# Stores later in SP's queue, resting rings, and three tiles for the experts' sums in a four-layer kernel

## The chip, the cores and the metric

The kernel runs on one core of a Trainium2 chip. The metric is the device time of one execution in microseconds (us); before the change its median over three runs is 5413.93 us. A difference of less than about 0.2% (11 us) can't be told from none.

The core has five engines that run side by side and wait for each other by semaphores: PE (TensorE, matmuls and transposes), DVE (VectorE), ACT (ScalarE), POOL (GpSimd) and SP (SyncE), which here only issues DMAs. Each takes its instructions strictly in the order in which the program put them. An instruction that has to wait holds up all that stand behind it on that engine. For SP this means: a DMA that waits for its data, or for its tile, holds up every DMA behind it, whatever those are for.

## What is computed

Four layers, each added to its input, on a tensor of 4 images, 384 channels and 48 x 48 places, all in float32. Each layer first normalises its input over 32 groups of channels.

```python
# layer 0: a selective scan over the 2304 places of an image
xz = xs @ in_proj_w.T;  xin, z = split(xz)
xin = silu(conv1d(xin) + conv_b)                    # 4 taps
dt, Bm, Cm = split(xin @ x_proj_w.T);  dt = softplus(dt @ dt_proj_w.T + b)
h_t = exp(dt_t * A) * h_(t-1) + dt_t * B_t * x_t    # 768 channels x 16 states
y_t = sum over states of h_t * C_t
out = layer_norm((y + xin * D) * silu(z) @ out_proj_w.T)
# layer 1: 1x1 conv, filter of 8x8 patches in Fourier space, 3x3 depthwise conv,
#          gelu(first half) * second half, 1x1 conv
# layer 2: 11x11 depthwise conv with kernels made from 4 points
# layer 3: 4 experts, each relu(w1 x + b1), then w2, weighted by a router's top 2
```

## The kernel before, in words

**Scans.** Layer 0 sets the frame. The 2304 places of an image are cut into five chunks (460 or 464 wide), so there are 20 chunks over the four images, numbered 0 to 19 here. A chunk has 6 blocks of 128 channels and 16 states, which makes 96 scans: 1920 in all. The program is written out slot by slot, one scan a slot, in a fixed order on each engine (`manual_schedule`). In slot u ACT makes a decay `da` (L942), POOL makes `bu` = u * B (L953) for slot u + 3, DVE scans (`scan`, L966), and either DVE (L986) or POOL (L995) multiplies by C into a tile `g`, which PE adds up by transposing it into `y` (L886). B and C of a state are 230 KB strips, broadcast to all partitions by DMA from a small DRAM tensor `bcd` (`spread`, L930): one of each every second slot, on SP's queue. B has three buffers and C four.

**What runs beside the scans.** Everything else is cut into tasks: Python generators that `yield` the kind of engine they need next. A `Lane` steps its tasks through the slots: at a `yield ("pool",)`, for example, a task goes on in the middle phase of a later slot. Each step takes at least one slot, so `wait(n)` lets n slots pass. A step can also ask that a `Ring` of tiles has one free. This planning happens when the program is built; what it yields is only the order of the instructions.

- `plan` places the tasks of layer 0 for each chunk: `load` of the next chunk's input (`xch`, L731, two buffers), `project` (PE product `pin` L749, ACT copy L762, three DVE sums L768 per block), `gate`, `out_proj`, `layer_norm`, and `residual`, which adds the result to the old chunk's `xch` tile (L1091), takes statistics, and stores it to `x1d` (L1095). The chunk to be loaded takes the tile that `residual` has just stored from.
- `early_z` computes z of images 3 and 2 ahead, in slots of image 0, and stores it to `zd` (L661).
- `later(b)` is layers 1 to 3 up to the router's scores of image b, and runs during the scans of image b + 1, started at slot 42 of that image. Its strips of layer 1 are in `finish_strip` (27 DVE taps L1415, three products L1447, store of `xr`), the bands of layer 2 in `load_band` (L1513) and `windows` (`xb`, L1578, stored to `x3d` at L1582), the router's input in `scores_of` (`xg`, L1649).
- `experts(b)` is layer 3 of image b: four experts, each 16 blocks of 144 places. A block loads `xe` from `x3d` (L1737) and, but for the first expert, the sum so far `ye` from the DRAM tensor `y3d` (L1740), makes two products on PE (`ph` and `pout`, L1750, 18 matmuls each in the trace) with a relu on ACT between (L1766), adds on DVE (L1782, or L1785 for the first expert, which adds in place to its `xe` tile), and stores back to `y3d`, or to `out` after the last expert (L1791). The tasks of an image come behind each other in a second lane.

All layer work of image 3, and whatever is left of image 2's experts, runs behind the last scan. There a chunk's slots are only steps of the lanes. Image 3's own experts come last, in `all_experts` (`ph` L1850, `pout` L1867), and nothing runs beside them.

**Rings.** `Ring(make, n)` hands out n tiles in turn. `done(k)` marks a tile as read, and `free()` tells the planner that the oldest tile is marked. It marks at the moment at which the program's next instruction may stand: for a tile that is stored, just behind the store's issue. The semaphores then see to it that a load into that tile waits on SP until the store has landed.

Of the kernel before, what the change touches and what calls it, by code (L numbers as in the profile page):

```python
# [9 lines left out]
F32 = mybir.dt.float32  # L10
# [6 lines left out]
P = 128  # L17
# [24 lines left out]


class Ring:


    def __init__(self, make, n):
        self.make, self.n, self.read = make, n, []

    def free(self, k=1):  # L50
        return all(self.read[: max(0, len(self.read) + k - self.n)])

# [5 lines left out]
    def done(self, k):  # L58
        self.read[k] = True

# [34 lines left out]
class Lane:  # L95
# [6 lines left out]

    def step(self, phase, slot, at=0):
        for task in self.active:
            if task.ended:
                continue
            kind, weight, ring, when = task.next
            if PHASE.get(kind, 1) != phase or task.after > slot:
                continue
            if weight and self.bound and self.meter.value + weight > self.meter.limit:  # L110
                continue
            if (ring and not ring[0].free(ring[1])) or (when and not when()):
                continue
# [29 lines left out]
def tile_layers(ctx: ExitStack, tc: tile.TileContext, a: dict, out: bass.AP):  # L143
# [31 lines left out]
    def group_norm(st, bank, mean, rstd, name):  # L175
# [14 lines left out]
        def to_channels(src, n, what):  # L190
            ps = bank(f"c{what}{name}")
            for ct in range(CT):
                nc.tensor.matmul(
                    ps[:, n * ct : n * ct + n], lhsT=gexp[:, bass.ts(ct, P)], rhs=src,
                    start=True, stop=True,
                )
            return ps[:, : n * CT]
# [15 lines left out]
    def group_norm_steps(st, ring, mean, rstd, name):  # L213
# [15 lines left out]
        def to_channels(src, n, what):  # L229
            ps, k = ring.take(f"c{what}{name}")  # L230
            for ct in range(CT):
                nc.tensor.matmul(
                    ps[:, n * ct : n * ct + n], lhsT=gexp[:, bass.ts(ct, P)], rhs=src,
                    start=True, stop=True,
                )
            return ps[:, : n * CT], k
# [179 lines left out]
    with ExitStack() as first:  # L416
# [142 lines left out]
        def scans(wk, mm, ring, meter, place, lanes, begin):  # L559
# [9 lines left out]
            def image_stats(b, ct, h):  # L569
                t = wk.tile([P, TT * C], F32, name=f"xs0_{b}_{ct}_{h}", tag="on", bufs=1)  # L570
                half = HW // 2
                nc.sync.dma_start(t[:, :half], a["x"][b, bass.ts(ct, P), bass.ts(h, half)])
                yield from wait(6)
                for k in range(3):
                    yield ("dve",)
                    nc.vector.bn_stats(stats0[:, b % 2, ct, h, k, :], t[:, bass.ts(k, LB)])

            def image_norm(b):
                yield from group_norm_steps(
                    stats0[:, b % 2].rearrange("p c h k s -> p c (h k) s"), ring,  # L580
                    mean0[:, b], rstd0[:, b], f"0_{b}",
                )
# [54 lines left out]
            def early_z(b, t, j):  # L637
# [21 lines left out]
                ring.done(r)  # L659
                yield ("pool",)  # L660
                nc.sync.dma_start(zd[b][bass.ts(j, P), bass.ds(starts[t], n)], z[:, :n])  # L661
# [62 lines left out]

            def load(i):
                (b, t), c = G[i], st[i]
                x = c["x"] = wk.tile(
                    [P, CT, DCONV - 1 + TM], F32, name=f"xch{b}_{t}", tag="xch", bufs=2
                )
                h = DCONV - 1 if t else 0  # L730
                nc.sync.dma_start(  # L731
                    x[:, :, DCONV - 1 - h : DCONV - 1 + CHUNKS[t]],
                    strip(a["x"][b], bass.ds(starts[t] - h, h + CHUNKS[t])),
                )
                return
                yield

# [336 lines left out]
            def residual(i, ct):  # L1074
# [18 lines left out]
                nc.vector.bn_stats(stats1[b % 2][:, ct, t, :], x)  # L1093
                yield ("pool",)
                nc.sync.dma_start(x1d[b][bass.ts(ct, P), bass.ds(starts[t], n)], x)  # L1095
# [172 lines left out]
        def later(b, ring, accr):  # L1268
# [10 lines left out]

            def slots(tag, shape, n):  # L1280

                return Ring(
                    lambda name: d["wk"].tile(shape, F32, name=name, tag=tag, bufs=n), n
                )
# [10 lines left out]
            def begin1():  # L1295
                wk = d["wk"] = stack.enter_context(tc.tile_pool(name=f"l1_{b}", bufs=2))
                d["w_in"] = wk.tile([P, CT, C], F32, name=f"w_in1_{b}", tag="w_in", bufs=1)
                nc.sync.dma_start(d["w_in"], per_channel(a["L1_w_inT"]))
                w = d["w_out"] = wk.tile([P, 2, C], F32, name=f"w_out1_{b}", tag="w_out", bufs=1)
                nc.sync.dma_start(w[:, 0, :], a["L1_w_outT"][:P, :])  # L1300
                nc.sync.dma_start(w[64:P, 1, :], a["L1_w_outT"][P:, :])
                mean = small.tile([P, CT], F32, name=f"mean1_{b}", tag="mean")
# [90 lines left out]
            def finish_strip(hb):  # L1393
# [46 lines left out]
                for ct in range(CT):  # L1440
                    yield ("pe", 1.3, (ring, 1))
                    ps, r = ring.take(f"pb{b}_{hb}_{ct}")
                    nc.tensor.matmul(  # L1443
                        ps[:, :LB], lhsT=w[:, 0, bass.ts(ct, P)], rhs=act[:, 0, :],
                        start=True, stop=False,
                    )
                    nc.tensor.matmul(  # L1447
                        ps[:, :LB], lhsT=w[64:P, 1, bass.ts(ct, P)], rhs=act[64:P, 1, :],
                        start=False, stop=True,
# [97 lines left out]
            def windows(ct, k, r, first, last, final):  # L1547
# [26 lines left out]
                if last:  # L1574
# [5 lines left out]
                    nc.vector.bn_stats(stats3[b % 2][:, ct, k, :], x[:, :n])  # L1580
                    yield ("pool",)
                    nc.sync.dma_start(x3d[b][of_band(ct, k)], x[:, :n])  # L1582
# [38 lines left out]

            xg = slots("xg", [P, CT, LB], 2)

# [64 lines left out]
        def experts(b, ring, rings):  # L1688
# [42 lines left out]
            def load3(s, e):  # L1731
                yield (
                    "pool", 0, None,
                    lambda: rings["xe"].free() and (not e or rings["ye"].free()),
                )
                x = take(("x", s, e), "xe", f"xe{b}_{s}_{e}")
                nc.sync.dma_start(x, strip(x3d[b], bass.ts(s, EB)))  # L1737
                if e:
                    y = take(("y", s, e), "ye", f"ye{b}_{s}_{e}")
                    nc.sync.dma_start(y, strip(y3d, bass.ts(s, EB)))  # L1740
                yield from wait(3)

            def block(s, e):
# [33 lines left out]
                yield ("late",)  # L1777
                key = ("y" if e else "x", s, e)
                x = d[key][0]
                if e:  # L1780
                    y = x.rearrange("p c t -> p (c t)")
                    nc.vector.tensor_add(y, ps[:, : CT * EB], y)  # L1782
                else:
                    for m in range(CT):
                        nc.vector.scalar_tensor_tensor(  # L1785
                            x[:, m, :], ps[:, bass.ts(m, EB)], b2_sum[:, m : m + 1],
                            x[:, m, :], ALU.add, ALU.add,
                        )
                ring.done(r)
                yield ("pool",)  # L1790
                nc.sync.dma_start(strip(out[b] if e == NE - 1 else y3d, bass.ts(s, EB)), x)  # L1791
                done(key)

# [104 lines left out]

        def of_experts(pool, sizes):
            for tag, n in sizes.items():  # L1900
# [4 lines left out]
                    ),  # L1905
                    n,
                )
# [13 lines left out]
        def begin(b):  # L1921
# [9 lines left out]
            first.enter_context(tc.tile_pool(name="experts", bufs=2)),  # L1931
            {"we": 1, "xe": 2, "ye": 2, "hr": 1},
        )
        with (
# [6 lines left out]
            at = place[0]  # L1941
            while not all(ring.read):
                at += 1
# [5 lines left out]
        with (  # L1949
# [135 lines left out]
```

## Time and profile before

The three runs took 5412.89, 5413.93 and 5417.67 us. The profile is of one further execution.

| what | us |
|---|---|
| median of the runs | 5413.93 |
| profiled execution | 5405.14 |
| its span, from first to last instruction | 5403.1 |
| scans, first to last | 86.5 to 4516.4 |
| mean granted TensorE clock, share of full | 0.919 |

How the queries are read. A row of waits names the engine and line that waited, the arrow to what ended the wait, then the total in us, the number of times and the longest. `SPq` is SP's queue, `DMA y3d<-ye` the transfer from the tile ye to y3d. In a timeline a row has start, duration, engine, line, operation, what it writes and reads and how many were merged, and in brackets the idle time before it with what ended it. The rows in tenths are 40 equal slices of the span.

DMAs on SP's queue that matter here, from the list of issues (us from issue to landing, median):

```profile
xe<-x3d SPq DMA_DIRECT2D x192, 216.0 KB, 2.8
ye<-y3d SPq DMA_DIRECT2D x144, 216.0 KB, 2.8
y3d<-ye SPq DMA_DIRECT2D x96, 216.0 KB, 2.2
...
x1d<-xch SPq DMA_DIRECT2D x48, 230.0 KB, 4.2
...
y3d<-xe SPq DMA_DIRECT2D x48, 216.0 KB, 2.7
out<-ye SPq DMA_DIRECT2D x48, 216.0 KB, 4.5
...
x3d<-xb SPq DMA_DIRECT2D x36, 240.0 KB, 3.2
xch<-in_x SPq DMA_DIRECT2D x12, 694.5 KB, 4.5
```

### The profile page before, as it was taken

What the parts mean: (1) busy time and instruction counts of PE and PEld (TensorE: products, weight loads), DVE (VectorE), ACT (ScalarE), POOL (GpSimd) and SP (SyncE); (2) the same over time, 40 slices, a digit from 0 to 9 for tenths busy, and PEclk for the clock granted to TensorE, in tenths of its full rate; (3) what the DMA queues carried; (4) which work ended last, traced back from release to release, by engine and by line L of the source; (5) the groups of instructions that cost most, each with busy time, mean ns of one, the idle gap of its engine ahead of it and who ended that gap; (6) DMA issues with size and microseconds to landing.
All of it is one profiled execution on the core that took longest, in us unless ns stands there. A gap on an engine that the chain in (4) does not pass through costs nothing. (4 is left out here: it accounts for less than half of the span.)

```text
span 5403.1 us, 82006 instructions
## 1 busy us (share of the span) xinstructions
PE 4646.1 (86%) x27796; PEld 3666.7 (68%) x27796; DVE 4067.1 (75%) x5581; ACT 2989.0 (55%) x6632; POOL 3363.1 (62%) x3020
## 2 busy tenths in 40 slices
PE   5898877787768988888889988888799988999899
PEld 3555545454446766765668867665678877889799
DVE  5998899889997888889887778798987875452200
ACT  3566655565547765565567745565477653335321
POOL 3788778886677788876678678775677783000000
PEclk8898987788879999998899999998899999999899
DMA  4565545443344555655566565655566573543210
GB/s 152 172 187 175 178 128 150 129 143 120 111 127 131 148 165 157 191 161 147 149 172 178 161 200 155 173 146 149 154 182 174 158 213 115 175 138 105 64 27 23
DMA packets 648873, 794.36 MB, mean 147 GB/s; under 512 B 60149, under 2 KB 642661, under 8 KB 648062
## 3 DMA queue, kind: packets, MB, share of 16 engines
q1 hardware_dynamic: 638148, 787.38, 49.9%
q8 instruction: 221, 3.62, 0.3%
q10 hardware_dynamic: 10298, 1.67, 0.2%
q14 instruction: 206, 1.69, 0.1%
HBM read 685.04 MB, written 103.81 MB: 146 GB/s over the span
## 5 line engine op out<-in xcount | busy, mean ns | idle before, releaser
L953 POOL TENSOR_TENSOR bu<-u,B 128x460 f32<-128x460 f32 (+1 forms) x1920 | 2227.0, 1170 | 795.5 <-DVE g L966 349.8
L942 ACT ACTIVATE da<-dt,a_neg 128x460 f32<-128x460 f32 (+1 forms) x1920 | 1242.4, 648 | 310.6 <-DVE g L986 185.6
L886 PE MATMUL y<-ident,g 128*115 128x128 f32 (+1 forms) x7680 | 1111.3, 292 | 192.5 <-DVE g L986 114.8
L886 PEld LDWEIGHTS y<-ident,g 128*115 128x115 f32 (+1 forms) x7680 | 991.2, 183 | 400.4 <-DVE g L986 140.5
L995 POOL TENSOR_TENSOR g<-g,C 128x460 f32<-128x460 f32 (+1 forms) x885 | 1030.0, 1164 | 246.8 <-ACT carry L980 244.3
L966 DVE TENSOR_TENSOR_SCAN da<-da,carry,bu 128x460 f32<-128x460 f32 (+1 forms) x828 | 971.7, 1174 | 122.2 <-ACT da L942 76.7
L966 DVE TENSOR_TENSOR_SCAN g<-da,carry,bu 128x460 f32<-128x460 f32 (+1 forms) x708 | 819.8, 1167 | 57.7 <-issue 18.8
L986 DVE TENSOR_TENSOR g<-da,C 128x460 f32<-128x460 f32 (+1 forms) x1035 | 656.4, 634 | 175.7 <-DMA C<-bcd 62.0
L980 ACT COPY carry<-da 128x1 f32<-128x1 f32 x828 | 130.3, 157 | 760.5 <-DVE g L986 758.0
L1750 PE MATMUL pout<-hr,we 128*128 128x144 f32 x3456 | 485.0, 297 | 51.5 <-ACT hr L1766 37.8
L1750 PE MATMUL ph<-xe,we 128*128 128x144 f32 x3456 | 484.7, 298 | 33.6 <-DMA xe<-x3d 18.9
L1750 PEld LDWEIGHTS pout<-hr,we 128*128 128x128 f32 x3456 | 456.3, 197 | 75.3 <-ACT hr L1766 47.9
L1750 PEld LDWEIGHTS ph<-xe,we 128*128 128x128 f32 x3456 | 459.4, 199 | 51.5 <-DMA xe<-x3d 13.7
L1557 PE MATMUL pc<-band,row 128*128 128x162 f32 (+14 forms) x3456 | 451.3, 284 | 11.2 <-ACT row L1544 10.9
L1557 PEld LDWEIGHTS pc<-band,row 128*128 128x128 f32 x3456 | 440.0, 194 | 16.6 <-ACT row L1544 11.9
L749 PE MATMUL pin<-xch,w_inx 128*128 128x463 f32 (+2 forms) x720 | 344.8, 621 | 55.1 <-DMA xch<-in_x 32.3
L1415 DVE SCALAR_TENSOR_TENSOR dw<-pad,w_dw,dw 128x384 f32<-128x384 f32 x576 | 348.0, 615 | 20.4 <-ACT pad L1390 9.6
L1037 PE MATMUL po<-w_out,zs 128*115 128x384 f32 (+1 forms) x960 | 342.2, 499 | 14.7 <-DVE ye L1782 9.3
L1766 ACT ACTIVATE hr<-ph,nb 128x144 f32<-128x144 f32 x576 | 176.2, 376 | 279.2 <-PE ph L1750 278.4
L1524 ACT ACTIVATE rep<-x,br,wr 128x192 f32<-128x192 f32 x576 | 273.7, 540 | 4.2 <-issue 4.2
L768 DVE SCALAR_TENSOR_TENSOR xc<-pin,conv_w,xc 128x460 f32<-128x460 f32 (+1 forms) x360 | 249.2, 692 | 30.7 <-ACT xc L762 18.5
L749 PEld LDWEIGHTS pin<-xch,w_inx 128*128 128x128 f32 x720 | 143.8, 213 | 179.8 <-issue 136.3
(211 smaller groups left out, 5979.2 us busy)
## 6 DMA issues: line engine op xcount, KB each, us to landing
B<-bcd SPq DMA_DIRECT2D x768, 230.0 KB, 3.6
C<-bcd SPq DMA_DIRECT2D x768, 230.0 KB, 4.0
B<-bcd SPq DMA_DIRECT2D x192, 232.0 KB, 3.8
C<-bcd SPq DMA_DIRECT2D x192, 232.0 KB, 4.3
xe<-x3d SPq DMA_DIRECT2D x192, 216.0 KB, 2.8
ye<-y3d SPq DMA_DIRECT2D x144, 216.0 KB, 2.8
y3d<-ye SPq DMA_DIRECT2D x96, 216.0 KB, 2.2
xs<-x1d SPq DMA_DIRECT2D x24, 576.0 KB, 5.2
```

The lines of the kernel that those rows point to most:

```text
L749: nc.tensor.matmul(ps[:, lo : halo + n], lhsT=w_inx[:, k, bass.ts(j, P)], rhs=c["x"][:, k, lo : halo + n], start=k == 0, stop=k == CT - 1,)
L886: nc.tensor.matmul(c["y", m][:w, bass.ts(k, P)], lhsT=src[:, bass.ts(k, w)], rhs=ident, is_transpose=True, start=c["terms", m] == 1 and k ...
L942: nc.scalar.activation(da[:, :n], c["dt", p][:, m % 2, :n], AF.Exp, scale=a_neg[:, m, s : s + 1])
L953: nc.gpsimd.tensor_mul(bu[:, :n], c["u", p][:, m % 2, :n], live["B", u // 2][:, :n])
L966: nc.vector.tensor_tensor_scan(here[:, :n], da[:, :n], bu[:, :n], last if t else nil[:, 0:1], ALU.mult, ALU.add,)
L986: nc.vector.tensor_mul(live["g", u][:, :n], live["h", u][:, :n], live["C", u // 2][:, :n])
L995: nc.gpsimd.tensor_mul(g[:, :n], g[:, :n], live["C", u // 2][:, :n])
L1037: nc.tensor.matmul(ps[:w, :C], lhsT=c["zs"][:, m, bass.ts(k, w)], rhs=w_out0[:, m, :], start=m == 0, stop=m == MT - 1,)
L1415: nc.vector.scalar_tensor_tensor(v, src, w_dw[:, ct, k : k + 1], v, ALU.mult, ALU.add)
L1524: nc.scalar.activation(rep[:, :, n, :, :].rearrange("p g r c -> p r g c"), rows.rearrange("p (r g c) -> p r g c", r=BR, c=BC), AF.Identity ...
L1557: nc.tensor.matmul(d["acc2"][0][:, : BANDS[k] * W].rearrange("p (h w) -> p h w", w=W)[:, lo - edges[k] : hi - edges[k], xlo:xhi], lhsT=d[" ...
L1750: nc.tensor.matmul(ps[:, bass.ts(m, EB)], lhsT=w[:, k, bass.ts(m, P)], rhs=of[:, k, :], start=k == 0, stop=k == CT - 1,)
```

## The change

A ring gets a `rest`: a tile counts as free only `rest` slots after its `done`. The rings of `early` and `xb` and the experts' `ye` in the scans rest two slots, `xg` and the experts' `xe` one. Stores of `zd`, `x1d`, `x3d` and of the experts' sums wait two or three slots, where they waited one, and the load of the next chunk waits two more. In the scans the experts have three `ye` tiles instead of two, and `xb` has four tiles instead of two. The first expert no longer adds in place to its `xe` tile but into a `ye` tile, which it stores; its `xe` tile is free after that sum. Behind the scans the experts' rings have no rest. Room in SBUF comes from two places: the second part of layer 1's `w_out` is kept once, in unused partitions of `gexp`, and `stats0` has one copy instead of two.

```diff
+CLOCK = [0]
 class Ring:
-    def __init__(self, make, n):
-        self.make, self.n, self.read = make, n, []
+    def __init__(self, make, n, rest=0):
+        self.make, self.n, self.read, self.rest = make, n, [], rest
     def free(self, k=1):
-        return all(self.read[: max(0, len(self.read) + k - self.n)])
+        return all(
+            v is not False and v + self.rest <= CLOCK[0]
+            for v in self.read[: max(0, len(self.read) + k - self.n)]
+        )
...
     def done(self, k):
-        self.read[k] = True
+        self.read[k] = CLOCK[0]
...
     def step(self, phase, slot, at=0):
+        CLOCK[0] = slot
...
-    gexp = const("gexp", [GROUPS, C], a["c_gexp"])
+    gexp = cp.tile([P, C], F32, name="gexp")
+    nc.sync.dma_start(gexp[:GROUPS, :], a["c_gexp"])
+    nc.scalar.dma_start(gexp[64:P, :], a["L1_w_outT"][P:, :])
...
-        stats0 = wp.tile([P, 2, CT, 2, 3, 6], F32, name="stats0")
+        stats0 = wp.tile([P, 1, CT, 2, 3, 6], F32, name="stats0")
...
             def early_z(b, t, j):
...
-                yield ("pool",)
+                yield from wait(2)
                 nc.sync.dma_start(zd[b][bass.ts(j, P), bass.ds(starts[t], n)], z[:, :n])
...
             def load(i):
+                yield from wait(2)
...
             def residual(i, ct):
...
-                yield ("pool",)
+                yield from wait(3)
                 nc.sync.dma_start(x1d[b][bass.ts(ct, P), bass.ds(starts[t], n)], x)
...
-                    n,
+                    n, 2,
...
-            xbs = slots("xb", [P, max(BANDS) * W], 2)
+            xbs = slots("xb", [P, max(BANDS) * W], 4, 2)
...
-                    yield ("pool",)
+                    yield from wait(2)
                     nc.sync.dma_start(x3d[b][of_band(ct, k)], x[:, :n])
...
-            xg = slots("xg", [P, CT, LB], 2)
+            xg = slots("xg", [P, CT, LB], 2, 1)
...
             def load3(s, e):
                 yield (
                     "pool", 0, None,
-                    lambda: rings["xe"].free() and (not e or rings["ye"].free()),
+                    lambda: rings["xe"].free() and rings["ye"].free(),
                 )
                 x = take(("x", s, e), "xe", f"xe{b}_{s}_{e}")
                 nc.sync.dma_start(x, strip(x3d[b], bass.ts(s, EB)))
+                y = take(("y", s, e), "ye", f"ye{b}_{s}_{e}")
                 if e:
-                    y = take(("y", s, e), "ye", f"ye{b}_{s}_{e}")
                     nc.sync.dma_start(y, strip(y3d, bass.ts(s, EB)))
-                yield from wait(3)
+                yield from wait(2)
...
-                            x[:, m, :], ps[:, bass.ts(m, EB)], b2_sum[:, m : m + 1],
+                            y[:, m, :], ps[:, bass.ts(m, EB)], b2_sum[:, m : m + 1],
                             x[:, m, :], ALU.add, ALU.add,
                         )
+                    done(("x", s, e))
                 ring.done(r)
-                yield ("pool",)
-                nc.sync.dma_start(strip(out[b] if e == NE - 1 else y3d, bass.ts(s, EB)), x)
-                done(key)
+                yield from wait(2)
+                nc.sync.dma_start(strip(out[b] if e == NE - 1 else y3d, bass.ts(s, EB)), y)
+                done(("y", s, e))
...
-            {"we": 1, "xe": 2, "ye": 2, "hr": 1},
+            {"we": 1, "xe": 2, "ye": 3, "hr": 1}, {"xe": 1, "ye": 2},
...
-            of_experts(wk, {"we": 2, "xe": 3, "ye": 3, "hr": 3})
+            of_experts(wk, {"we": 2, "xe": 3, "ye": 3, "hr": 3}, {})
```

More of the change, by code (lines that the diff above doesn't have):

```diff
@@ L193, in to_channels @@
                 nc.tensor.matmul(
-                    ps[:, n * ct : n * ct + n], lhsT=gexp[:, bass.ts(ct, P)], rhs=src,
+                    ps[:, n * ct : n * ct + n], lhsT=gexp[:GROUPS, bass.ts(ct, P)], rhs=src,
                     start=True, stop=True,
@@ L232, in to_channels @@
                 nc.tensor.matmul(
-                    ps[:, n * ct : n * ct + n], lhsT=gexp[:, bass.ts(ct, P)], rhs=src,
+                    ps[:, n * ct : n * ct + n], lhsT=gexp[:GROUPS, bass.ts(ct, P)], rhs=src,
                     start=True, stop=True,
@@ L575, in image_stats @@
                     yield ("dve",)
-                    nc.vector.bn_stats(stats0[:, b % 2, ct, h, k, :], t[:, bass.ts(k, LB)])
+                    nc.vector.bn_stats(stats0[:, 0, ct, h, k, :], t[:, bass.ts(k, LB)])
             def image_norm(b):
                 yield from group_norm_steps(
-                    stats0[:, b % 2].rearrange("p c h k s -> p c (h k) s"), ring,
+                    stats0[:, 0].rearrange("p c h k s -> p c (h k) s"), ring,
                     mean0[:, b], rstd0[:, b], f"0_{b}",
@@ L734, in load @@
                 )
-                return
-                yield
             def project(i, j):
@@ L1278, in put, with slots @@
                 tasks.append(task)
-            def slots(tag, shape, n):
+            def slots(tag, shape, n, rest=0):
                 return Ring(
-                    lambda name: d["wk"].tile(shape, F32, name=name, tag=tag, bufs=n), n
+                    lambda name: d["wk"].tile(shape, F32, name=name, tag=tag, bufs=n), n, rest
                 )
@@ L1298, in begin1 @@
                 nc.sync.dma_start(d["w_in"], per_channel(a["L1_w_inT"]))
-                w = d["w_out"] = wk.tile([P, 2, C], F32, name=f"w_out1_{b}", tag="w_out", bufs=1)
-                nc.sync.dma_start(w[:, 0, :], a["L1_w_outT"][:P, :])
-                nc.sync.dma_start(w[64:P, 1, :], a["L1_w_outT"][P:, :])
+                w = d["w_out"] = wk.tile([P, C], F32, name=f"w_out1_{b}", tag="w_out", bufs=1)
+                nc.sync.dma_start(w, a["L1_w_outT"][:P, :])
                 mean = small.tile([P, CT], F32, name=f"mean1_{b}", tag="mean")
@@ L1443, in finish_strip @@
                     nc.tensor.matmul(
-                        ps[:, :LB], lhsT=w[:, 0, bass.ts(ct, P)], rhs=act[:, 0, :],
+                        ps[:, :LB], lhsT=w[:, bass.ts(ct, P)], rhs=act[:, 0, :],
                         start=True, stop=False,
@@ L1447, in finish_strip @@
                     nc.tensor.matmul(
-                        ps[:, :LB], lhsT=w[64:P, 1, bass.ts(ct, P)], rhs=act[64:P, 1, :],
+                        ps[:, :LB], lhsT=gexp[64:P, bass.ts(ct, P)], rhs=act[64:P, 1, :],
                         start=False, stop=True,
@@ L1777, in block @@
                 yield ("late",)
-                key = ("y" if e else "x", s, e)
-                x = d[key][0]
+                y = d["y", s, e][0]
                 if e:
-                    y = x.rearrange("p c t -> p (c t)")
-                    nc.vector.tensor_add(y, ps[:, : CT * EB], y)
+                    of = y.rearrange("p c t -> p (c t)")
+                    nc.vector.tensor_add(of, ps[:, : CT * EB], of)
                 else:
@@ L1897, in tile_layers, with of_experts @@
         place = [0]
-        def of_experts(pool, sizes):
+        def of_experts(pool, sizes, rest):
             for tag, n in sizes.items():
@@ L1905, in of_experts @@
                     ),
-                    n,
+                    n, rest.get(tag, 0),
                 )
@@ L1941, in tile_layers @@
             at = place[0]
-            while not all(ring.read):
+            while not ring.free(ring.n):
                 at += 1
```

## The prediction

> **What bounds the kernel now.** I began with the page's totals and slices: no engine is full over the span, so the bound has to be read by stage.
>
> ```profile
> PE 4646.1 (86%) x27796; PEld 3666.7 (68%) x27796; DVE 4067.1 (75%) x5581; ACT 2989.0 (55%) x6632; POOL 3363.1 (62%) x3020
> DVE  5998899889997888889887778798987875452200
> POOL 3788778886677788876678678775677783000000
> ```
>
> The 1920 scans (one is a "slot") run from 86.5 to 4516.4 us, 2.31 us a slot; there DVE and POOL are both 7 to 9 tenths busy. Behind 4516 POOL has nothing to do. From the stretches: 4516 to 4912 (layers 1 of the last image beside image 2's experts) has PE busy 376 of 396 us; 5100 to 5403 is PE alone, untouched by the change. In the scans PE, DVE and POOL lie close: 3125 to 3344 has PE 193, DVE 173, POOL 171 of 219 us. So what counts there is idle time of DVE and POOL. The waits say who causes it; first SP's own queue in the scans (0 to 4516):
>
> ```profile
> SPq L1740 <- DMA y3d<-ye: 185.9, 64, 7.5
> SPq L1791 <- DVE ye L1782: 160.8, 52, 7.6
> SPq L1737 <- DMA y3d<-xe: 138.5, 38, 8.0
> SPq L1513 <- DMA x3d<-xb: 119.2, 39, 5.6
> ...
> SPq L1740 <- DMA out<-ye: 105.9, 28, 7.2
> SPq L661 <- ACT carry L980: 104.3, 36, 7.2
> SPq L731 <- DMA x1d<-xch: 72.8, 19, 5.3
> SPq L1582 <- DVE xb L1578: 68.6, 28, 6.1
> ...
> SPq L1791 <- DVE xe L1785: 46.6, 26, 5.3
> ```
>
> SP stands 1003 us (the sum of these nine) on a store whose data isn't made, or on a load whose tile is still being stored. Behind it in the same queue are the B and C strips of the scan. The timeline shows it, once per expert block:
>
> ```profile
> 4414.77 0.39 SPq L1791 DMA_DIRECT2D out<-ye  x1
> 4415.20 1.38 SPq L1737 DMA_DIRECT2D xe<-x3d  x1
> 4420.96 0.36 SPq L1740 DMA_DIRECT2D ye<-y3d  x1
> 4421.72 0.33 SPq L930 DMA_DIRECT2D B<-bcd  x1
> ```
>
> From 4416.6 to 4421.0 SP issues nothing; DVE's product at 4419.02 had stood idle 3.46 us for its C, and POOL's bu at 4416.97 1.69 us for B. Over 1961 to 4516, where experts run:
>
> ```profile
> DVE g L986 <- DMA C<-bcd: 58.4, 25, 6.1
> ```
>
> POOL idles 93.8 us for B in that stretch, mostly where DVE isn't waiting for it.
>
> **The change, part by part.** I read where each instruction lands from the built order of both kernels; a slot is placed in SP's queue by the B load beside it.
>
> *Stores later, rings resting, three ye tiles.* In the scans, all 92 ye loads that wait for a ye store stood in the store's own slot; now 71 do, each 2 or more slots behind. The 36 xe loads that waited for y3d<-xe are gone (expert 0 writes a ye tile), 39 xb loads become 2 at 4 slots, 18 xch loads move from 0 to 2 slots or more. Two slots are 4.2 us in the experts' stage (2.10 each from 4314 to 4516); the stores land in 2.2 (y3d<-ye), 4.5 (out<-ye) and 3.2 us (x3d<-xb). The Trainium skill, "DMA: Bandwidth & Descriptors", Anatomy of one DMA, prices a transfer at 2.0 us + bytes/436 GB/s: 2.5 us for these 216 KB, so by the rule no wait is left. By the row out<-ye leaves 0.3 us x 28 = 8 us on SP, which its queue hides. I take the row: nearly all 1003 us of SP's standing goes, only the tile xr (61.0 us) stays. What that is worth is DVE's idle time, not SP's: 58.4 for C, and about 9 us of scans late behind a bu that was late for B, makes 67. Another engine is close behind in each stage, so some comes back as another wait: ends 25 (most is retaken by ACT's da, 65.1 us of DVE idle now, and PE) and 95 (POOL's B idle counts as well where POOL sets the pace). I take 70% of 67: **-47 us**, near the row.
>
> *The next chunk's xch load goes later.* x1d stores move from slots 35, 37, 39 to 37, 39, 41, and the load from 39 to 43 in 18 of 19 chunks; the projection that reads it stays at slot 45 on PE, its ACT copy and its three DVE sums (slot 47) behind it in their queues. This is the change's own new wait. Now:
>
> ```profile
> 932.40 0.38 SPq L1095 DMA_DIRECT2D x1d<-xch  x1
> 936.64 0.38 SPq L731 DMA_DIRECT2D xch<-in_x  x1
> 937.08 0.48 SPq L930 DMA_DIRECT2D B<-bcd  x1
> 937.66 0.38 SPq L930 DMA_DIRECT2D C<-bcd  x1
> 939.50 0.32 SPq L930 DMA_DIRECT2D B<-bcd  x1
> 939.87 0.42 SPq L930 DMA_DIRECT2D C<-bcd  x1
> ...
> 942.01 0.32 SPq L930 DMA_DIRECT2D B<-bcd  x1
> ```
>
> The load already waited for its store, and goes at 936.6; in the new order it stands behind the pair of 939.5, so at 940.3, 3.7 us later. PE's pin started at 941.18, when it landed (PE idle 2.67); it would start at 944.9, and DVE's sum, at 946.37 now with 0.90 idle, at 949.9. Everything behind that on DVE, the scan of slot 48 first, waits: 3.7 us. Done so for each chunk (new issue = the later of POOL's second bu of slot 45 + 0.85 us and the third store's landing; less PE's and DVE's slack), chunks 2 to 10 lose 1.6, 1.8, 3.8, 3.7, 1.8, 0, 2.8, 0.9, 1.2, and chunks 11 to 19 nothing, since SP was so late there that the load went at DVE's slot 42 to 45 anyway. Sum **+18 us**; ends 0 (SP ahead of this) and 72 (4.0 us in all 18).
>
> *More blocks in the scans.* Of image 2's 64 expert blocks 57.7 had PE work behind the last scan, now 51.9. About six blocks move into the scans: 6 x 0.6 us DVE (L1782) is 3.6, and 27 us of PE, which has 10 to 30 us idle in each chunk; **+5** (0 to 15).
>
> *Behind the scans.* Six blocks less are 6 x 2 x 2.21 = 26.5 us of PE. But the experts now end during layer 1's strip 4 of the last image, where they ended behind strip 5. So layer 1's end stands alone: 27 taps of 0.615 us for the last strip are 16.6 us of DVE, with gelu and three products some 35 us from strip 4's product to the next norm, against 56 now (4853.7 to 4910). Up to strip 4 there are 5.1 blocks more beside it than before, +22.5. Together +22.5 - 21 = about 0; the start gains 8, since two rounds like this one, store then load into one tile, fall away:
>
> ```profile
> 4506.48 4.19 DMA y3d<-xe
> 4510.69 2.71 DMA xe<-x3d
> ```
>
> **-8** (-26 if all of PE's time counts, +8 if the lone strip is slower).
>
> *The rest.* Early z is spread over slots 63 to 351 (58 to 290 before) with the same work, and is through before slot 480; slots 288 to 480 without it took 1.96 us, 96 to 288 with it 2.01. gexp's second half is one ACT-queue DMA hidden by the 1152 KB loads at the start; four 96 KB w_out loads go. stats0's single copy meets no reader, as image 0's norm is long done. Nothing for these.
>
> Sum: -47 + 18 + 5 - 8 = -32. The profiled execution took 5405.1 us (span 5403.1), so 5373; the runs' median, 5413.9, is 8.8 above it, so I forecast 5414 - 32 = **5382**.
>
> A rule speaks against this: the skill's "Perfetto Trace Analysis", Identifying the Most-Contended Engine, says to optimise the engine of highest occupancy first. That is PE (86%), and PE waits only 16.2 us on xe loads in 1961 to 4516, so the rule prices the gain at 16 and, with pins +18 and blocks +5, the sum at about 0. I follow the row: the scan's chain is in order on DVE, and DVE's 3.46 us at 4419 were lost with PE free.
>
> **Rivals.** (1) *The freed time is retaken*: DVE then waits for ACT's da or PE instead; for it speaks PE's 219 us of 235 in 4079 to 4314. Gain 25 instead of 47: -10, 5404. (2) *The xch load decides, slower*: at slot 45 of 18 chunks PE, ACT and DVE stand behind a later load. The rest of the change nets -50, so this decides from 50/18 = 2.8 us a chunk; at the full 4.0 it is +72, time 5436. For it: chunks 4 and 5 work out at 3.7. Against: SP's lateness in chunks 11 to 19. (3) *POOL's idle counts too*: 95 instead of 47 and pins at 5: -93, 5321; for it POOL's 93.8 us, against it DVE waits little for bu. (4) That the loads still stand behind their stores is ruled out by the order.
>
> **Chances.** Forecast 0.47 (own range 5354 to 5404), rival 1 0.18, rival 2 0.20, rival 3 0.15. The range 5330 to 5436 reaches most of rival 2 and part of 3. Within 0.2% (11 us, what a measurement can tell) lie rival 1 and a little of the forecast's edge, less rival 1's own edge: 0.17; slower 0.20; faster 0.63.
>
> **What would show it.** In the new profile: SP's waits of ye, xe, xb loads on stores near zero in the scans; DVE's idle for C under 20 us; the last scan ending near 4492; PE's wait on xch up from 46 us, with DVE's sums idle at slot 47; fewer than 52 blocks behind the last scan and layer 1's last strip alone. Wrong if C's wait stays, or if slots 40 to 56 of chunks 2 to 10 grow by more than 3 us each.

## The result and the profile after

The changed kernel takes **5445.5 us** (median of 6 runs, 5434.4 to 5452.9), beside 5413.4 for the kernel before on the same chip: a ratio of 1.0066 (95% interval 1.0049 to 1.0083), some 32 us slower. The forecast was 5382, its range ended at 5436. The profiled execution has a span of 5440.7 us; its scans run from 87.9 to 4582.7, 64.9 us longer than before, and what lies behind them takes 858.0 instead of 886.7. So the loss is in the scans, and part of it is won back behind them.

The page's totals and slices, in the order shown of before:

```profile
PE 4661.6 (86%) x27796; PEld 3665.8 (67%) x27796; DVE 4063.9 (75%) x5581; ACT 2983.3 (55%) x6632; POOL 3362.4 (62%) x3020
...
DVE  5988888888997788889897777889897776353200
...
POOL 3778778787676778876677677876677786000000
```

DVE and POOL do the same work as before within 4 us. What grew is idle time in between. SP's own queue over the scans:

```profile
SPq L940 <- POOL bu L963: 2537.3, 843, 14.1
SPq L847 <- ACT xd L843: 137.2, 20, 42.8
SPq L1746 <- PE ph L1759: 92.1, 33, 6.6
SPq L1746 <- DVE ye L1793: 83.2, 32, 5.3
...
SPq L1749 <- DMA y3d<-ye: 35.3, 24, 3.9
...
SPq L1591 <- DVE xb L1587: 18.3, 17, 2.4
SPq L743 <- DMA x1d<-xch: 15.5, 8, 4.1
```

Here the change does what was forecast: the ye loads' 186 us on their stores are 35, the 138 us of the xe loads on y3d<-xe are gone, and SP mostly stands at the first row: the next B strip waiting for its buffer. New is that the xe loads stand 175 us for the readers of their tiles (third and fourth row). DVE's idle time for C, summed over the scans, went from 62 us to 2.6. It didn't help. The groups of the chunk's projection, PE's product and DVE's sum, before:

```profile
L749 PE MATMUL pin<-xch,w_inx 128*128 128x463 f32 (+2 forms) x720 | 344.8, 621 | 55.1 <-DMA xch<-in_x 32.3
L768 DVE SCALAR_TENSOR_TENSOR xc<-pin,conv_w,xc 128x460 f32<-128x460 f32 (+1 forms) x360 | 249.2, 692 | 30.7 <-ACT xc L762 18.5
```

and after:

```profile
L759 PE MATMUL pin<-xch,w_inx 128*128 128x463 f32 (+2 forms) x720 | 349.4, 628 | 101.6 <-DMA xch<-in_x 86.2
L778 DVE SCALAR_TENSOR_TENSOR xc<-pin,conv_w,xc 128x460 f32<-128x460 f32 (+1 forms) x360 | 249.6, 693 | 111.1 <-ACT xc L772 58.9
```

The number behind the second bar is the idle time just before these instructions, and the row's end says what ended most of it. PE stood 32.3 us for xch before and stands 86.2 us now; DVE's idle time before the sum went from 30.7 to 111.1 us, 80 us more, which is more than the scans lost in all.

The place is the one that the prediction showed at 932 to 942 us, in chunk 4. SP's queue there now:

```profile
961.33 0.38 SPq L940 DMA_DIRECT2D C<-bcd  x1
961.76 0.42 SPq L1105 DMA_DIRECT2D x1d<-xch  x1
964.98 0.32 SPq L940 DMA_DIRECT2D B<-bcd  x1
965.39 0.38 SPq L940 DMA_DIRECT2D C<-bcd  x1
965.88 0.38 SPq L743 DMA_DIRECT2D xch<-in_x  x1
967.48 0.32 SPq L940 DMA_DIRECT2D B<-bcd  x1
```

The load stands behind the next B and C pair. PE's product and DVE's sum of that chunk, first before:

```profile
941.18 4.09 PE L749 MATMUL pin<-xch,w_inx 128*128 128x460 f32 x6 [2.67 <-DMA xch<-in_x]
...
946.37 2.16 DVE L768 SCALAR_TENSOR_TENSOR xc<-pin,conv_w,xc 128x460 f32<-128x460 f32 x3 [0.90 <-ACT xc L762]
```

and after:

```profile
969.77 1.17 DVE L976 TENSOR_TENSOR_SCAN g<-da,carry,bu 128x464 f32<-128x464 f32 x1
971.66 4.94 PE L759 MATMUL pin<-xch,w_inx 128*128 128x460 f32 x6 [7.68 <-DMA xch<-in_x]
...
977.70 2.16 DVE L778 SCALAR_TENSOR_TENSOR xc<-pin,conv_w,xc 128x460 f32<-128x460 f32 x3 [6.76 <-ACT xc L772]
979.78 1.18 DVE L976 TENSOR_TENSOR_SCAN da<-da,carry,bu 128x464 f32<-128x464 f32 x1
```

DVE ends a scan at 970.94 and does nothing until 977.70: 6.76 us, where it was 0.90. That is 5.86 us for this chunk. Measured from the scan of slot 34 in both traces, the load was issued 3.76 us later (the prediction had 3.7). But then it took 5.78 us from issue to PE's start, where it had taken 4.54: 1.24 more. And the six matmuls themselves went slower, 4.94 us instead of 4.09: 0.85 more. These three terms, 3.76 + 1.24 + 0.85, are what DVE lost. All this is chunk 4 alone.

The 0.85 us come from PE's clock. The stretch of the six matmuls, before:

```profile
941.18:942.05 0.87, 0.87 (x3) 1.00 1.06 373
942.05:945.46 3.41, 3.41 (x7) 0.50 0.64 212
```

and after:

```profile
971.66:976.60 4.94, 4.94 (x7) 0.50 0.40 109
```

The columns are the stretch and its length, PE's busy time with the number of its matmuls (those that only touch the stretch are counted too), then the granted TensorE clock, the DMA share (of packets that start in the stretch, so it can pass 1) and GB/s. Before, PE began at full clock and was halved 0.87 us into the product, which ended at 945.27; after, it was at half clock throughout. Counted in time at full clock both are the same work: 0.87 + 3.22/2 = 2.48 us, and 4.94/2 = 2.47. In chunk 17 of the changed kernel the six ran at a clock of 1.00 and took 2.57:

```profile
4030.66 2.57 PE L759 MATMUL pin<-xch,w_inx 128*128 128x463 f32 x6 [2.93 <-DMA xch<-in_x]
```

The Trainium skill, "TensorE: Matmul & The Clock Gate", Part 1, says that PE's clock is halved after an idle window of about 3.4 us, and comes back after as long of steady work. The half clock behind 7.68 us of idle time agrees with it. But before, 2.67 us of idle time were enough, and 2.93 us in chunk 17 were not, so here the length of the idle time alone doesn't decide. The page also calls the window free-running, which would make it matter where in it the idle time falls; no run here tests that.

### The profile page after: what moved, and what is told of

Same layout as the page of the kernel before. It is cut to its first block, busy times and chain, and to the rows that moved or that the text cites. A ratio compares the mean times of both kernels' runs of the same rounds, so it can differ in the third digit from the quotient of the medians.

```text
span 5440.7 us, 81940 instructions
## 1 busy us (share of the span) xinstructions
PE 4661.6 (86%) x27796; PEld 3665.8 (67%) x27796; DVE 4063.9 (75%) x5581; ACT 2983.3 (55%) x6632; POOL 3362.4 (62%) x3020
## 5 line engine op out<-in xcount | busy, mean ns | idle before, releaser
L1759 PE MATMUL ph<-xe,we 128*128 128x144 f32 x3456 | 473.5, 293 | 7.1 <-DVE zs L1033 3.4
L759 PE MATMUL pin<-xch,w_inx 128*128 128x463 f32 (+2 forms) x720 | 349.4, 628 | 101.6 <-DMA xch<-in_x 86.2
L778 DVE SCALAR_TENSOR_TENSOR xc<-pin,conv_w,xc 128x460 f32<-128x460 f32 (+1 forms) x360 | 249.6, 693 | 111.1 <-ACT xc L772 58.9
```

The lines of the kernel that those rows point to most:

```text
L759: nc.tensor.matmul(ps[:, lo : halo + n], lhsT=w_inx[:, k, bass.ts(j, P)], rhs=c["x"][:, k, lo : halo + n], start=k == 0, stop=k == CT - 1,)
L1759: nc.tensor.matmul(ps[:, bass.ts(m, EB)], lhsT=w[:, k, bass.ts(m, P)], rhs=of[:, k, :], start=k == 0, stop=k == CT - 1,)
```

## Experiments

Two theories stood at the start. **P**: the cost is the later xch load alone, larger than the +18 of the forecast, and the rest of the change is a gain. **R**: the time that SP's freed queue gives is retaken by other waits all over the scans, and the load is a small part. The first four kernels ran beside the kernel before at 5412.3 us, the next four at 5411.3, the last two at 5413.7, each group on a chip of its own, so times of different groups are set beside each other here.

**1. The load back.** The changed kernel, with the load and the stores of its tile where they stood before:

```diff
             def load(i):
-                yield from wait(2)
+                yield from ()
...
             def residual(i, ct):
...
-                yield from wait(3)
+                yield ("pool",)
                 nc.sync.dma_start(x1d[b][bass.ts(ct, P), bass.ds(starts[t], n)], x)
```

> The changed kernel with two waits taken out again: the x1d stores one slot behind their sums and the next xch load right behind the third, as before; rings, experts and bands as changed. Theory P (the later xch load is the cost: PE's first projection waits, ACT's copy and DVE's three sums stand behind it in their queues): DVE's idle in slots 40 to 52 falls from 135 us to 75 or so, scans end near 4520 instead of 4583, time about 5385, under the kernel before since the experts' stalls are gone and six blocks left the tail. Theory R (what the freed C and B loads gave is retaken by ACT and PE everywhere, and the new order of the lanes costs by itself): the time stays at 5430 or more; slots 40 to 48 explain at most 20 us.

Measured: **5354.4 us**, ratio to before 0.9897 (0.988 to 0.9913). The two lines cost 91 us in the changed kernel, more than the 60 that were expected, and without them it is 58 us faster than before. Chunk 4 of this kernel:

```profile
940.18 0.38 SPq L743 DMA_DIRECT2D xch<-in_x  x1
940.62 0.48 SPq L940 DMA_DIRECT2D B<-bcd  x1
...
944.63 3.78 PE L759 MATMUL pin<-xch,w_inx 128*128 128x460 f32 x6 [2.46 <-DMA xch<-in_x]
```

The load is ahead of the pair again, and PE starts 4.45 us behind its issue. Summed by groups of eight slots, the changed kernel is 82.7 us longer in the scans than this one, and slots 40 to 48 alone make 83.0 of it. Behind the last scan it is 15.0 us longer (858.0 and 843.0). That is more than the 91 in all, because the profile of this kernel is of the fastest of its four runs. The scans are 17.8 us shorter than before, and what lies behind them is 843.0 us, 43.7 less than before. Theory P holds for the scans.

**2. The load alone.** The kernel before, with the two delays and nothing else of the change:

```diff
             def load(i):
+                yield from wait(2)
...
-                return
-                yield
...
             def residual(i, ct):
...
-                yield ("pool",)
+                yield from wait(3)
                 nc.sync.dma_start(x1d[b][bass.ts(ct, P), bass.ds(starts[t], n)], x)
```

> The kernel before with those two waits alone: x1d stores two slots later, next xch load behind two more slots. Theory P: slower by 50 to 70 us (about 5470), with 5 to 7 us more in slots 40 to 48 of chunks 1 to 8 and PE's wait for xch near 90 us; in chunks 9 to 19 less, as SP stands on the experts' stores anyway. Theory R: at most 20 us slower, 5430.

Measured: 5530.6 us, ratio 1.0219 (1.0202 to 1.0236), 118 us slower, where 50 to 70 were expected. PE stands 160.0 us for xch before pin, up to 20.0 at a time. That SP's standing at the experts' loads delays the load still further here is likely, but wasn't tested by itself. So the two parts of the change aren't independent, and the change's other half softens this one: 91 instead of 118.

**3. Which of the two delays.** The changed kernel with only the load's own wait taken out (e4), and with only the stores put back (e7):

```diff
             def load(i):
-                yield from wait(2)
+                yield from ()
```

> The changed kernel with only the load's own two slots taken out: the stores stay two slots later, and the xch load is issued right behind the third store. The load must wait for that store's landing of about 4 us, so it goes at about the same time as in the changed kernel. Theory P with the store as its cause: 5445 within 10 us, PE's wait for xch stays near 90 us, and SP's wait on x1d<-xch is back at 70 us. Theory P with the load's two slots as its cause: 5400 or less. Theory R: no change.

```diff
             def residual(i, ct):
...
-                yield from wait(3)
+                yield ("pool",)
```

> The kernel after with the residual stores back at one slot, the load's own wait of two slots left in. Two slots of the load on top of late stores cost 5445.5 - 5415.5 = 30 us (after against e4_store_late). If the price is one per slot of lateness, the two slots cost about 30 here too: 5385. If there is slack and only the last slots of lateness hurt, the two first slots are nearly free: 5355 to 5365. Idle of PE before pin for xch: 30 us by the first, under 20 by the second.

Measured: 5415.5 (ratio 1.0004, 0.9997 to 1.0011) and 5376.6 (0.994, 0.9924 to 0.9957). From the kernel with neither, the load's wait alone costs 22 us, the stores' alone 61, and the load's wait on top of the stores' 30. For e4 neither of the outcomes named in advance came, for e7 the time lay between them. The load cannot start before the stores of its tile have landed: with the late stores alone SP stands 75.4 us for them at the load, as expected. Chunk 4 of the kernel with the load's wait alone:

```profile
955.52 0.38 SPq L940 DMA_DIRECT2D C<-bcd  x1
956.13 0.38 SPq L743 DMA_DIRECT2D xch<-in_x  x1
...
961.91 4.17 PE L759 MATMUL pin<-xch,w_inx 128*128 128x460 f32 x6 [3.73 <-DMA xch<-in_x]
```

Measured from the scan of slot 36, the load goes at 12.06 us here and at 12.12 in experiment 1: no later at all. Only its place differs, behind the pair instead of ahead of it, and PE starts 5.78 us after the issue instead of 4.45. So 1.3 us of the price in this chunk go with the place in the queue, not with the time of issue. In chunks 1 to 4 this kernel's load, always right behind a pair, takes 1.3 to 2.0 us longer from issue to PE than experiment 1's.

**4. The projection later.** The changed kernel with PE's six projections moved later (the first by three slots, the next four by two or one, the last not at all), which gives the late load its time back (e5), and the same on the kernel of experiment 1 (e6):

```diff
-                            put(45 + 3 * j, ("x", more, j), lambda j=j: project(more, j),
+                            put(48 + 5 * j // 2, ("x", more, j), lambda j=j: project(more, j),
```

> The changed kernel with the next chunk's six projections starting at slot 48 instead of 45 and 2.5 slots apart instead of 3 (they end at slot 60 as before). Theory P: the load has landed when PE reaches the first projection; PE's wait for xch falls under 15 us, DVE's idle in slots 40 to 52 falls by 60 us or more, time about 5375 to 5385. Theory R: within 10 us of the changed kernel, 5445.

> The kernel after with the chunk's load and its residual stores back where they were before (as in e1_load_back, 5354.4) and, besides, the four projections at slots 48, 50, 53, 55 (as in e5_pin_late, 5369.2). If the projection's slot matters only because the load lands late (theory P), nothing is left to gain once the load is early: PE's idle for xch falls from 13 to about 0 and the time is 5340 to 5360. If the later slot is worth something by itself, 5300 to 5335. If the later projections crowd the next chunk's beginning, over 5370.

Measured: 5369.2 (ratio 0.9924, 0.9907 to 0.9941) and 5355.9 (0.9894, 0.9871 to 0.9918). The load may stay where the change put it: with a later reader, PE's idle time for xch falls from 86.2 to 2.5 us, and 76 of the 91 us come back. With the load early there is nothing to gain from it (5354.4 and 5355.9). So the cost in the scans is the distance between the load and its reader, not the load's place beside other work: e5's scans are even 5.6 us shorter than experiment 1's.

The 15 us that don't come back lie behind the last scan, and go with the late stores. The three kernels that have them need 858.0 (the change), 856.6 (e4) and 865.4 us (e5) there; the kernels with the stores back need 842.1 (e7), 843.0 (experiment 1) and 848.9 (e6). In each of the three PE stands for layer 1's last strip, in the changed kernel:

```profile
4935.01 0.91 PE L1456 MATMUL pb<-act,gexp 64*128 64x384 f32 x2
4944.43 1.62 PE L1452 MATMUL pb<-act,w_out 128*128 128x384 f32 x2 [8.50 <-DVE act L1446]
4945.97 1.65 PE L1456 MATMUL pb<-act,gexp 64*128 64x384 f32 x2
```

In e4 and e5 it is 8.15 us, and in the other three no such wait is there. Behind it the same two matmuls take 1.65 us instead of 0.91, at a granted clock of 0.50. How the late stores lead to this is open.

Over the variants of the changed kernel that keep the reader at slot 45 the time goes with PE's idle time for xch before pin:

| kernel | PE idle for xch, us | time, us |
|---|---|---|
| neither delay (1) | 13.0 | 5354.4 |
| load's wait (3) | 31.0 | 5376.6 |
| stores' wait (3) | 57.0 | 5415.5 |
| both: the change | 86.2 | 5445.5 |

From the first row to the last that is 91.1 us for 73.2, or 1.24 us of time for each us that PE stands there.

**5. What gains the other 58 us.** Four kernels from that of experiment 1. In the first the experts' part is undone: two ye tiles, no rest for xe and ye, the first expert's sum in xe, the store at the next step.

```diff
-                    lambda: rings["xe"].free() and rings["ye"].free(),
+                    lambda: rings["xe"].free() and (not e or rings["ye"].free()),
...
-                y = d["y", s, e][0]
+                key = ("y" if e else "x", s, e)
+                x = d[key][0]
...
-                yield from wait(2)
-                nc.sync.dma_start(strip(out[b] if e == NE - 1 else y3d, bass.ts(s, EB)), y)
-                done(("y", s, e))
+                yield ("pool",)
+                nc.sync.dma_start(strip(out[b] if e == NE - 1 else y3d, bass.ts(s, EB)), x)
+                done(key)
...
-            {"we": 1, "xe": 2, "ye": 3, "hr": 1}, {"xe": 1, "ye": 2},
+            {"we": 1, "xe": 2, "ye": 2, "hr": 1}, {},
```

> e1_load_back with the experts' part undone: two ye tiles, no rest for xe and ye, the first expert's sum in its xe tile, the store at the next POOL step, three slots after the load. If the experts carry what the change gains, all 58 us come back: about 5410, with some six more blocks behind the last scan (about 880 us there) and DVE waiting for C again by 20 us and more outside slots 40 to 52. If the gain is that of the xb, x3 and early z parts, it stays near 5365, with 845 to 855 us behind the last scan.

Measured: 5413.0, ratio 1.0004 (0.9993 to 1.0014). All 58 us are the experts'; the xb, xg and early z parts and the room made for the tiles, taken together, show none. Of the two places named for them, the one behind the last scan was only partly met: 862.6 us there, not 880; the scans gave the larger part. DVE's idle time for C came back to 42 us, but only 14 of them lay outside slots 40 to 52, where 20 and more were expected.

The second undoes the xb part:

```diff
-            xbs = slots("xb", [P, max(BANDS) * W], 4, 2)
+            xbs = slots("xb", [P, max(BANDS) * W], 2)
...
-                    yield from wait(2)
+                    yield ("pool",)
                     nc.sync.dma_start(x3d[b][of_band(ct, k)], x[:, :n])
```

> e1_load_back with the xb part undone: two xb tiles, no rest, the x3d store at the next POOL step. If the experts carry the gain, this costs little: 5355 to 5365. If the standing of SP at the xb loads and stores (119 and 69 us in the kernel before) is what cost the scans, 5375 to 5400, the loss in the scans and not behind them.

Measured: 5348.9, ratio 0.9887 (0.987 to 0.9904), not to be told from experiment 1. Yet SP's queue stands again, over the scans:

```profile
SPq L1522 <- DMA x3d<-xb: 115.3, 39, 5.9
SPq L1591 <- DVE xb L1587: 78.3, 33, 5.5
```

194 us of SP's standing at xb, where experiment 1 has 13.5 in the second row. They cost nothing that the time shows: in the profiles the scans are 12.9 us longer and what lies behind them is 6.4 shorter.

The third and fourth split the experts' part: three ye tiles without rests (e10), and the rests with two ye tiles (e11).

```diff
-            {"we": 1, "xe": 2, "ye": 3, "hr": 1}, {"xe": 1, "ye": 2},
+            {"we": 1, "xe": 2, "ye": 3, "hr": 1}, {},
```

> e1_load_back with three ye tiles, but without the rest of the xe and ye rings in the scans: a load may again stand in the step of its tile's store. If SP's standing is what the experts' part took away (my term of -47), SP stands at ye and xe loads again for hundreds of us and the 58 us come back: about 5410. If the third tile and the earlier take, which let a block's loads run ahead of the block before, carry the gain, it stays at 5350 to 5370.

```diff
-            {"we": 1, "xe": 2, "ye": 3, "hr": 1}, {"xe": 1, "ye": 2},
+            {"we": 1, "xe": 2, "ye": 2, "hr": 1}, {"xe": 1, "ye": 2},
```

> e1_load_back with two ye tiles instead of three in the scans, the rest of both rings kept. A ye tile is then out of use for longer in each round, so fewer blocks are done in the scans. If the third tile carries the gain: more PE work behind the last scan (880 us and more there) and 5400 to 5440. If freeing SP is enough: 5355 to 5375.

Measured: 5364.2 (ratio 0.9911, 0.9891 to 0.9931) and 5426.9 (1.0021, 1.0006 to 1.0036). Without the rests 10 us are lost, within the two intervals. This test is weaker than was expected of it: SP stood less than "hundreds of us" more, perhaps since the third tile alone already takes most loads away from their stores. The rows of e10 over the scans:

```profile
SPq L1746 <- PE ph L1759: 226.3, 56, 10.9
SPq L1749 <- DMA y3d<-ye: 115.0, 34, 5.9
```

In experiment 1 they are 95.8 and 24.9 us: 221 us more of standing for about 10 us. The third tile, on the other hand, is worth 72 us where the rests are kept (5426.9 - 5354.4). Two tiles without rests, in experiment e8, take 5413.0. Where the third tile acts is seen from the experts' two products on PE, counted up to the last scan and behind it; first experiment 1:

```profile
0.00:4499.10 4499.10, 702.22 (x5055) 666.04 (x5056) 0.91 0.55 160
4499.10:4899.10 400.00, 241.76 (x1860) 232.72 (x1858) 0.98 0.49 145
```

then two tiles with rests:

```profile
0.00:4495.80 4495.80, 639.91 (x4395) 605.25 (x4396) 0.91 0.54 157
```

The number of matmuls is in brackets behind PE's time. A block is 36 matmuls, so 660 fewer are 18 blocks that didn't fit beside the scans. The scans themselves end at nearly the same time, and what lies behind takes 932.9 us instead of 843.0. In this pair a block beside the scans costs next to nothing; behind them it costs PE's full time.

## Why the prediction was wrong

**The term that failed is the +18 of "The next chunk's xch load goes later".** It measured 91 us against the rest of the change; in the profiles 83 of it lie in slots 40 to 48 and 15 behind the last scan. The mechanism and the order of the queue were right; the size was off for four reasons.

- *The issue was put too early, and what comes behind it was held constant.* In chunk 4 the time of issue was right (3.76 us later, 3.7 forecast), but the transfer then took 1.24 us longer and PE's matmuls 0.85. In chunk 3 the sum had a loss of 1.8 us, though PE had stood 2.57 us for the load and DVE 0.79 before its sum; the load was issued 4.15 us later. In chunks 2 to 10, against experiment 1, it was issued 2.8 to 9.7 us later (from the scan of slot 34), and PE's six matmuls took 40.5 us in all where experiment 1 had 27.9. The sum had 17.6 us for these chunks; slots 40 to 48 grew by 42.8 against the kernel before and are 49.0 longer than in experiment 1. Why the issue times fell short isn't shown.
- *Chunk 1 was left out.* It lost 7.6 us.
- *Chunks 11 to 19 were put at nothing, "since SP was so late there that the load went at DVE's slot 42 to 45 anyway".* That lateness was what another part of the same change removes. With it removed, the load in these chunks goes at slot 40 to 43 (experiment 1), and with the delays at 43 to 46. They lost 26.5 us. Against the kernel before this part doesn't show, as it cancels there: a gain of one part was spent by another.
- *Behind the last scan the late stores were put at nothing.* They cost some 15 us there (experiment 4).

The upper end that the prediction gave, 72 us from 4.0 us in 18 chunks, was too low too: 83 in 18 chunks is 4.6. Rival 2, that the load decides from 2.8 us a chunk, is what happened, at a price above the one named.

**The -47 for SP's freed queue was more than twice too large.** DVE's idle time for C did vanish, as forecast, and of the nine rows with SP's 1003 us 113 are left. But of the 58 us for C in chunks 9 to 19, 38 lay in slots 40 to 52. In the changed kernel the wait for the projection took their place there. With the load put back, DVE's idle time in those slots of those chunks falls by 46.5 us against the kernel before, while in the other slots it rises by 30: ACT's da takes 11.6 of it, PE's y 6.2 and pout 7.0. The scans are 17.8 us shorter net, with the six more blocks among them; with 1.5 us for the blocks (below) that makes -19. The step that failed is "I take 70% of 67": under 30% of it stayed. Rival 1, "the freed time is retaken", had -25 for this term and was near. That SP's standing itself is no measure, as the prediction said, is borne out: 194 us of it at xb were worth nothing, and 221 us at the experts' loads about 10. The fit that was weighed here, from the Trainium skill, "DMA: Bandwidth & Descriptors", Anatomy of one DMA, is given there for the path of gpsimd, and these transfers are SP's. The prediction took the row, so nothing rests on it.

**The +5 for more blocks in the scans was in its range, and on the high side.** 18 fewer blocks shortened the scans by only 4.4 us in the profiles, which makes 1.5 for six.

**The -8 behind the scans was too small.** It is -29 in the changed kernel and -44 with the load back. The count of blocks was right (57.7 to 51.9). The products' time behind the scans, before:

```profile
4516.40:4926.40 410.00, 273.09 (x2070) 262.41 (x2070) 0.97 0.49 141
```

and after:

```profile
4582.70:4992.70 410.00, 241.63 (x1860) 232.63 (x1858) 0.96 0.48 141
```

are 210 matmuls less, some six blocks, and 31.5 us, where the sum had 26.5. The wrong step was the 21 us set against it for "layer 1's end stands alone". It does stand alone in the changed kernel, for the 8.50 us shown above, but other idle time fell away: PE's idle time behind the scans is 50.8 us before, 50.2 after, and 40.5 with the load back. The near end of that range, -26 "if all of PE's time counts", was the case.

With the measured terms, -19 + 91 + 1 - 44 = +29, against +32 from the medians.

The signs that the prediction named were good ones. SP's waits on stores nearly gone, C under 20, fewer than 52 blocks behind the scans and layer 1's last strip alone: these came. The last scan ended at 4582.7, not near 4492. And the sign of failure came: slots 40 to 56 of chunks 2 to 10 were to grow by more than 3 us each, and grew by 4.9 to 7.8 in seven of the nine. The rule of the most contended engine, which was weighed against the row of C, put the sum at about 0, nearer than the forecast. That was luck, as the two parts that decided, +91 and -58, are not in it. It was also misread: the same section says that the busy share of matmuls is no good measure for TensorE, and names the share of the peak rate and that of the weight loads instead. Here the latter is PEld's 68%, under DVE's 75%. By it the rule points to DVE, as the row did.

## What to carry to other kernels

When a transfer is moved back, measure the distance to its reader and pay for everything behind the issue: the place in the queue, the transfer beside its new neighbours, the reader's engine after a longer rest. If the transfer must move, move its reader too: the one-line shift of the projection won back 76 of 91 us, all that the scans had lost. And where a change removes a delay in one place, redo the slack of its other parts with that delay gone; a standing DMA queue was no measure of time to win here, while one more tile in a ring whose tiles rest, which lets whole blocks of work move beside a longer stage, was worth 72 us.

The version to keep is that of experiment 1: the whole change but for the two delays around the xch load, at 0.9897 of the time before.

## What the runs showed of the hardware

- A load of 694.5 KB issued at the same point of the scan started its reader 4.45 us later when it was ahead of a pair of 230 KB strips in the queue, and 5.78 us later when it stood right behind one.
- After 7.68 us of idle time PE did six float32 matmuls of 460 columns in 4.94 us at a granted clock of 0.50. After 2.46 us of idle time (experiment 1) the same six took 3.78, the first 1.18 us at a clock of 1.00 and the rest at 0.50. After 2.93 us, in chunk 17 of the changed kernel, six of 463 columns took 2.57 at 1.00.
